# Attention and layer 1 of a graph network: two-part float32r tables beside another split of the mask and layernorm work

## The chip, the cores and the metric

One of the eight cores of a Trainium2 chip runs the whole program. Time is the device time of one execution in microseconds (us), and lower is better. A core has a matrix engine (TensorE, PE in the profile; its weight loads are PEld), a vector engine (VectorE, DVE), an activation engine (ScalarE, ACT), a general engine (GpSimd, POOL) and queues that issue transfers (SP, ACT and POOL).

## The reference

Sixteen graphs (B = 16) of 1024 nodes with 128 features pass through four layers, each with a residual addition and a layernorm. The change touches layers 0 and 1 and every layernorm.

```
# layer 0: masked attention
v = relu(x @ Wv.T + bv);  q = relu(x @ Wq.T + bq);  k = relu(x @ Wk.T + bk)
scores = einsum('bih,bjh->bij', q, k)
h = clip(scores * mask, 0.0, CLAMP_HI) - NEG_PENALTY * (1.0 - mask)
out = softmax(h, axis=2) @ v
# layer 1: maximum over the neighbours j of i
p = x @ (W1 - W2);  q = x @ W2
out = max_j relu(p[i] + q[j] + b) * adj[i, j]
# layer 2: a GIN layer.  layer 3: the adjacency is thinned row by row (dilation),
# then three SAGE layers with batch norms and a last linear map
# after each layer: x = layernorm(x + out)
```

The masks are the adjacency matrix itself, of zeros and ones. The thinning of layer 3 depends on the adjacency alone, and each row depends on the rows before it.

## The kernel before, in words

The program has two stages. The first, `layers_012`, computes layers 0 to 2 and, spread between their instructions, the thinning (`dilation`). The second, from the pools `xpool` and `sb` on, runs layer 3 batch by batch, four times over the sixteen graphs, and ends each graph with the last layernorm (called at L594).

In the first stage the outer loop runs over the graphs b. The spine of it is `max_conv(b)`, layer 1. A maximum over neighbours isn't a matrix product, so the kernel makes it one by tables. The 1024 neighbours are cut into 147 groups of seven (`NG`, `GS`). For each group, VectorE builds all 128 maxima over subsets of the seven values of `q`, for 21 groups at a time (`sub`, L270); TensorE transposes three groups at a time into `pt` (L277), and ScalarE copies them out as `table` (L279). The product of `lit` and the adjacency (`pm`, L284, bf16) tells which subset each node has as neighbours, and ScalarE turns it into a one-hot matrix `hot` (L286). The product of table and `hot` picks the maximum (`product`, L150, called by `look_up`, two halves of 512 columns in float32), and VectorE folds it into `best` (L262). So there are 16 x 147 = 2352 look-ups. A look-up is written one group late: `pm` and `hot` of group g stand before the look-up of group g-1. `pm` has one buffer of two PSUM banks, `pg` shares two such buffers with the other wide products.

After each group `between(g)` is called. It advances three generators. `dilation` gets 1400 pieces spread evenly over the 2352 groups: in each of eight blocks of 128 rows, 16 pieces that bring the block's rows up to date (a load of `E` by GpSimd's queue, L340; transposes and comparisons, L353 and L354), 127 steps of some ten small VectorE instructions that each need the one before (L374 to L387), 16 counts on ScalarE (L396), and 16 ranks (a scan of 1024 elements on VectorE, L413, an activation, L414, and a comparison, L416). `gin(b-1)`, layer 2, advances in the first 30 groups. `attention(b+1)`, layer 0, advances every tenth group from 40 on, one tile of 128 rows at a time.

One attention tile does this: GpSimd makes `off`, one where there is no edge (L219, bf16, from the adjacency rows `An`). TensorE multiplies q with the negated k (L222; GpSimd negates `kT` at L207) and adds 2^100 times `off` by a bf16 product with the diagonal matrix `penalty` (L223). VectorE clips and takes the row minimum in one instruction (L227), ScalarE takes the exponential (L229), TensorE transposes and multiplies with v, and VectorE scales and adds the residual (L242).

`layernorm` (L153 on) takes statistics of eight tiles on VectorE (L156), combines their halves by nine small GpSimd instructions (L161 to L169, the last a power), and normalises by eight GpSimd instructions (L171). It is called three times per graph in the first stage and once per graph at the end.

A scheduler orders each engine's instructions when the program is built; it follows program order where nothing stands against it. Each engine then runs its own in that order.

Of the kernel before, what the change touches and what calls it, by code (L numbers as in the profile page):

```python
# [23 lines left out]

F32 = mybir.dt.float32
BF = mybir.dt.bfloat16
U8 = mybir.dt.uint8  # L30
AF = mybir.ActivationFunctionType
ALU = mybir.AluOpType
# [4 lines left out]
P = 128  # L37
# [6 lines left out]
LOWEST = -(2.0**100)  # L44
MAGIC = 2.0**23
CLAMP_HI = 90000000000000.0
PENALTY = 2.0**100
LN_EPS = 1e-5


# [11 lines left out]
def tile_graph_layers(ctx: ExitStack, tc, a, out):  # L62
# [9 lines left out]
    def wide(name, tag="wide", bufs=2):  # L72
        return psum.tile([P, N], F32, tag=tag, name=name, bufs=bufs)

# [5 lines left out]
    make_identity(nc, ident)  # L80
    ident_b = consts.tile([P, P], BF, name="ident_b")
    make_identity(nc, ident_b)
    penalty = consts.tile([P, P], BF, name="penalty")
    nc.vector.tensor_scalar_mul(penalty, ident, PENALTY)
    ones = consts.tile([P, P], F32, name="ones")
    nc.vector.memset(ones, 1.0)
    ones_b = consts.tile([P, P], BF, name="ones_b")
# [31 lines left out]
    nc.vector.tensor_scalar_add(eps1, eps1, 1.0)  # L119


    mask_u = consts.tile([B, N], U8, name="mask_u")
    nc.sync.dma_start(out=mask_u, in_=a["nodemask"])
    half_mask = consts.tile([B, N], F32, name="half_mask")
    nc.vector.tensor_scalar(half_mask, mask_u, 0.5, None, op0=ALU.mult)
    nm = consts.tile([P, T, B], F32, name="nm")
    half_nm = consts.tile([P, T, B], F32, name="half_nm")
    pm = bank("pm")
# [23 lines left out]

    def layernorm(dst, src):  # L153
        st = small.tile([P, T, 6], F32, name="ln_st")
        for t in range(T):
            nc.vector.bn_stats(out=st[:, t, :], in_=src[:, t, :])  # L156

        mv = small.tile([P, 4, T], F32, name="ln_mv")
        mean, apart, var, rs = (mv[:, i, :] for i in range(4))
        gp = nc.gpsimd  # L160
        gp.tensor_add(mean, st[:, :, 1], st[:, :, 4])  # L161
        gp.tensor_sub(apart, st[:, :, 1], st[:, :, 4])  # L162
        gp.tensor_scalar(mean, mean, 0.5, None, op0=ALU.mult)  # L163
        gp.tensor_mul(apart, apart, apart)  # L164
        gp.tensor_add(var, st[:, :, 2], st[:, :, 5])  # L165
        gp.tensor_scalar(var, var, 1.0 / D, LN_EPS, op0=ALU.mult, op1=ALU.add)  # L166
        gp.tensor_scalar(apart, apart, 0.25, None, op0=ALU.mult)  # L167
        gp.tensor_add(var, var, apart)  # L168
        gp.tensor_tensor(rs, var, mhalf, op=ALU.pow)  # L169
        for t in range(T):  # L170
            gp.tensor_scalar(dst[:, t, :], src[:, t, :], mean[:, t:t + 1], rs[:, t:t + 1],  # L171
                             op0=ALU.subtract, op1=ALU.mult)

    def split(pool, src, left):

# [17 lines left out]
    def layers_012():  # L193
# [6 lines left out]
        def attention(b, An):  # L200
# [3 lines left out]
            kT = w4.tile([P, N], F32, name="kT")  # L204
            for w, bias, dst in ((WqT, bq, qT), (WkT, bk, kT)):
                nc.scalar.activation(dst, product(w, xT, "pqk"), AF.Relu, bias=bias)
            nc.gpsimd.tensor_scalar_mul(kT, kT, -1.0)  # L207
            v = w4.tile([P, T, D], F32, name="v")
            pv = wide("pv").rearrange("p (t d) -> p t d", d=D)
            for t in range(T):  # L210
# [3 lines left out]
            yield  # L214
            y = w4.tile([P, T, D], F32, name="y")
            for t in range(T):

                off = w4.tile([P, N], BF, name="off", tag="pen")
                nc.gpsimd.tensor_scalar(off, An[:, t, :], -1.0, 1.0, op0=ALU.mult, op1=ALU.add)  # L219
                psc = wide("psc")  # L220
                for s in halves:
                    nc.tensor.matmul(psc[:, s], qT[:, t * P:(t + 1) * P], kT[:, s], start=True, stop=False)  # L222
                    nc.tensor.matmul(psc[:, s], penalty, off[:, s], start=False, stop=True)  # L223
                e = w4.tile([P, N], F32, name="e", bufs=2)

                top = small.tile([P, 1], F32, name="top")
                nc.vector.tensor_scalar(e, psc, -CLAMP_HI, None, op0=ALU.max, op1=ALU.min, accum_out=top)  # L227
                total = small.tile([P, 1], F32, name="total")
                nc.scalar.activation(e, e, AF.Exp, bias=top, scale=-1.0, accum_out=total)  # L229
                eT = w4.tile([P, T, P], F32, name="eT")  # L230
                for h in range(2):
                    p = bank("pe")
                    for c in range(4):
                        nc.tensor.transpose(p[:, c * P:(c + 1) * P],
                                            e[:, (4 * h + c) * P:(4 * h + c + 1) * P], ident)
                    nc.scalar.copy(eT[:, 4 * h:4 * h + 4, :].rearrange("p c i -> p (c i)"), p)
                pav = bank("pav")
                for c in range(T):
                    nc.tensor.matmul(pav[:, :D], eT[:, c, :], v[:, c, :], start=(c == 0), stop=(c == T - 1))
                share = small.tile([P, 1], F32, name="share")  # L240
                nc.vector.reciprocal(share, total)
                nc.vector.scalar_tensor_tensor(y[:, t, :], pav[:, :D], share, X[b][:, t, :],  # L242
                                               op0=ALU.mult, op1=ALU.add)
                yield
# [3 lines left out]
        def max_conv(b, AT, between):  # L248
# [5 lines left out]
            qg = q.rearrange("o (g s) -> o g s", s=GS)  # L254
            best = w4.tile([P, N], F32, name="best")

            def look_up(g, table, hot):
                pg = product(table, hot, "pg")
                if g == 0:
                    nc.vector.tensor_copy(best, pg)  # L260
                else:
                    nc.vector.tensor_max(best, best, pg)  # L262

            last = None
            for g0 in range(0, NG, TG):
# [6 lines left out]
                for g in range(g0, g0 + TG):  # L272
                    at = (g - g0) % 3
                    if at == 0:
                        pt = bank("pt")
                        for k in range(3):
                            nc.tensor.transpose(pt[:, k * P:(k + 1) * P], sub[:, g - g0 + k, :], ident)  # L277
                        table = w2.tile([P, 3, P], F32, name="table", bufs=3)
                        nc.scalar.copy(table.rearrange("s g o -> s (g o)"), pt[:, :3 * P])  # L279
                    c, r = divmod(g, GC)  # L280
                    rows = min(CH, N - c * CH)
                    pm = wide("pm", "subset", 1)
                    for s in halves:
                        nc.tensor.matmul(pm[:, s], lit[:rows, r, :], AT[:rows, c, s], start=True, stop=True)  # L284
                    hot = w2.tile([P, N], F32, name="hot", bufs=2)
                    nc.scalar.activation(hot, pm, AF.Relu, bias=one_less)  # L286
                    if last is not None:
                        look_up(*last)
                    last = g, table[:, at, :], hot
                    between(g)  # L290
            look_up(*last)
            nc.vector.tensor_add(best, best, product(Wd, xT, "pp"))
# [43 lines left out]
        def dilation():  # L336
            for k in range(T):
# [32 lines left out]
                for n in range(P - 1):  # L370
                    mine = Dg[:, n, :]
                    m = slice(k * P + n, k * P + n + 1)
                    rank1 = small.tile([B, P], F32, name="rank1")
                    nc.vector.tensor_tensor_scan(rank1, mine, mine, before[:, n:n + 1], op0=ALU.add, op1=ALU.max)  # L374
                    sc = small.tile([B, 5], F32, name="sc")
                    half, h1, at, every, at2 = (sc[:, i:i + 1] for i in range(5))
# [3 lines left out]
                    nc.vector.scalar_tensor_tensor(at, half, 5.5, h1, op0=ALU.is_gt, op1=ALU.mult)  # L380
                    nc.vector.scalar_tensor_tensor(every, half, 1.0, at, op0=ALU.is_gt, op1=ALU.is_gt)
                    nc.vector.tensor_scalar(at2, at, 2.0, -1.0, op0=ALU.mult, op1=ALU.add)
                    hit = small.tile([B, P], F32, name="hit")
                    nc.vector.tensor_scalar(hit, rank1, at, every, op0=ALU.is_equal, op1=ALU.max)  # L384
                    nc.vector.scalar_tensor_tensor(hit, rank1, at2, hit, op0=ALU.is_equal, op1=ALU.max)  # L385
                    nc.vector.tensor_mul(hit, hit, mine)
# [236 lines left out]
```

## Time and profile before

| | |
|---|---|
| median of 3 runs | 9722.24 us (9721.92 to 9728.73) |
| the profiled execution | 9721.92 us |
| its span, first to last instruction | 9720.1 us |
| PE busy | 8365.7 us (86%), 29288 instructions |
| DVE busy | 7624.2 us (78%), 16197 instructions |
| ACT busy | 4286.9 us (44%), 5170 instructions |
| POOL busy | 1095.8 us (11%), 1423 instructions |
| mean granted TensorE clock | 0.932 |
| end of the loop over max_conv | about 7816 us |

Busy time counts an engine's instructions once where they overlap. A product in float32 shows as two records for each 512 columns (so L150 has 9408 for the look-ups). [...]records of one line overlap; the distance of their starts is the better price. A group of instructions is given with its count, its busy time, the mean of one in ns, and the idle time of the engine before them with what ended it. A wait is given as the engine and line that waited, the engine and line it waited for, the total in us, how often, and the longest.

### The profile page before, as it was taken

What the parts mean: (1) busy time and instruction counts of PE and PEld (TensorE: products, weight loads), DVE (VectorE), ACT (ScalarE), POOL (GpSimd) and SP (SyncE); (2) the same over time, 40 slices, a digit from 0 to 9 for tenths busy, and PEclk for the clock granted to TensorE, in tenths of its full rate; (3) what the DMA queues carried; (4) which work ended last, traced back from release to release, by engine and by line L of the source; (5) the groups of instructions that cost most, each with busy time, mean ns of one, the idle gap of its engine ahead of it and who ended that gap; (6) DMA issues with size and microseconds to landing.
All of it is one profiled execution on the core that took longest, in us unless ns stands there. A gap on an engine that the chain in (4) does not pass through costs nothing. (4 is left out here: it accounts for less than half of the span.)

```text
span 9720.1 us, 86636 instructions
## 1 busy us (share of the span) xinstructions
PE 8365.7 (86%) x29288; PEld 4084.1 (42%) x29288; DVE 7624.2 (78%) x16197; ACT 4286.9 (44%) x5170; POOL 1095.8 (11%) x1423
## 2 busy tenths in 40 slices
PE   7989898999899989898989898989898967778774
PEld 4444444444444444444444444444444433334333
DVE  4998599869886988699859986998699958845454
ACT  3445544554465445444554455445544621122221
POOL 1010101010101010101010101010101010101116
PEclk8999999999999999999999999999999978889886
DMA  3010201020102010201020102010200057733332
GB/s 47 1 22 19 35 1 22 19 37 1 22 20 39 1 22 20 40 1 22 19 43 1 22 18 46 1 22 18 47 1 11 11 159 201 200 115 130 130 130 75
DMA packets 317237, 435.20 MB, mean 45 GB/s; under 512 B 105445, under 2 KB 156792, under 8 KB 316662
## 3 DMA queue, kind: packets, MB, share of 16 engines
q1 hardware_dynamic: 219696, 295.75, 9.2%
q0 software_dynamic: 92560, 132.72, 8.8%
q8 instruction: 230, 3.77, 0.2%
q10 hardware_dynamic: 4534, 1.19, 0.1%
q14 instruction: 217, 1.78, 0.1%
HBM read 461.64 MB, written 119.54 MB: 60 GB/s over the span
## 5 line engine op out<-in xcount | busy, mean ns | idle before, releaser
L150 PE MATMUL pg<-hot,table 128*128 128x512 f32 x9408 | 4548.7, 605 | 134.4 <-DVE best L262 42.8
L286 ACT ACTIVATE hot<-pm,one_less 128x1024 f32<-128x1024 f32 x2352 | 2617.1, 1113 | 2235.1 <-PE pm L284 2080.4
L262 DVE TENSOR_TENSOR best<-best,pg 128x1024 f32<-128x1024 f32 x2336 | 2828.8, 1211 | 534.5 <-PE pg L150 530.4
L150 PEld LDWEIGHTS pg<-hot,table 128*128 128x128 f32 x9408 | 1729.4, 191 | 1770.3 <-issue 1137.5
L284 PE MATMUL pm<-AT,lit 126*128 126x512 bf16 x4704 | 1437.2, 385 | 190.9 <-ACT hot L286 101.3
L284 PEld LDWEIGHTS <-lit 126*128 126x128 bf16 x4704 | 461.0, 99 | 1099.8 <-issue 1067.1
L279 ACT COPY table<-pt 128x384 f32<-128x384 f32 x784 | 373.3, 477 | 816.5 <-PE pt L277 811.5
L219 POOL TENSOR_SCALAR off<-An 128x1024 bf16<-128x1024 bf16 x128 | 164.2, 1283 | 3578.7 <-PE psc L223 3183.0
L277 PE MATMUL pt<-ident,sub 128*128 128x128 f32 x2352 | 410.8, 283 | 178.3 <-DVE sub L270 88.6
L189 PE MATMUL pagg<-m,part 128*128 128x512 bf16 x2304 | 529.0, 382 | 34.9 <-DVE inv L530 25.4
L277 PEld LDWEIGHTS pt<-ident,sub 128*128 128x128 f32 x2352 | 304.4, 146 | 516.6 <-issue 270.2
L374 DVE TENSOR_TENSOR_SCAN rank<-Dg,before 16x128 f32<-16x128 uint8 x1016 | 498.4, 491 | 27.2
L270 DVE TENSOR_TENSOR sub<-sub,q 128x21 f32<-128x21 f32 (+6 forms) x784 | 434.9, 555 | 49.3 <-ACT q L252 43.9
L387 DVE TENSOR_TENSOR Dg<-Dg,hit 16x127 uint8<-16x127 uint8 (+63 forms) x1016 | 454.2, 447 | 24.5
L189 PEld LDWEIGHTS <-part 128*128 128x128 bf16 x3072 | 298.2, 98 | 394.9 <-issue 53.4
L385 DVE SCALAR_TENSOR_TENSOR hit<-rank,sc,hit 16x128 f32<-16x128 f32 x1016 | 348.1, 343 | 25.6
L557 PE MATMUL pl<-w_L_gnn_Wl,hT 128*128 128x128 f32 x768 | 199.1, 367 | 178.6 <-ACT hT L581 113.2
L178 ACT CAST part<-left 128x1024 bf16<-128x1024 f32 x128 | 133.7, 1044 | 482.9 <-DVE left L180 482.8
L384 DVE TENSOR_SCALAR hit<-rank,sc 16x128 f32<-16x128 f32 x1016 | 342.7, 337 | 0.0
L532 DVE RECIPROCAL inv<-inv 128x1024 f32<-128x1024 f32 x48 | 314.3, 6548 | 19.3 <-ACT inv L531 19.3
L560 DVE SCALAR_TENSOR_TENSOR x<-pl,nm,x 128x128 f32<-128x128 f32 x384 | 129.5, 337 | 252.2 <-PE pl L557 161.4
L171 POOL TENSOR_SCALAR X<-y,ln_mv 128x128 f32<-128x128 f32 x384 | 319.4, 848 | 5.2
(172 smaller groups left out, 8512.2 us busy)
## 6 DMA issues: line engine op xcount, KB each, us to landing
m<-kept SPq DMA_DIRECT2D x32, 2048.0 KB, 9.4
An<-in_adj_dram POOLq DMA_DIRECT2D x16, 2048.0 KB, 14.3
removed<-gone SPq DMA_DIRECT2D x128, 256.0 KB, 2.0
m<-in_adjT_dram POOLq DMA_DIRECT2D x16, 2048.0 KB, 13.6
gone_all<-removed SPq DMA_DIRECT2D x16, 2048.0 KB, 9.7
kept<-m SPq DMA_DIRECT2D x16, 2048.0 KB, 14.2
AT<-in_adjT_dram POOLq DMA_DIRECT2D x16, 2016.0 KB, 14.6
hidden<-r SPq DMA_DIRECT2D x48, 512.0 KB, 3.8
```

The costliest lines, as they stand in the source:

```text
L150: nc.tensor.matmul(p[:, s], lhsT, rhs[:, s], start=True, stop=True)
L189: nc.tensor.matmul(p[:, s], parts[k][:, c, :], m[:, c, s], start=(c == 0 and k == 0), stop=(c == T - 1 and k == 2))
L262: nc.vector.tensor_max(best, best, pg)
L270: nc.vector.tensor_max(sub[:, :, n:2 * n], sub[:, :, 0:n], qg[:, g0:g0 + TG, k:k + 1].to_broadcast([P, TG, n]))
L277: nc.tensor.transpose(pt[:, k * P:(k + 1) * P], sub[:, g - g0 + k, :], ident)
L279: nc.scalar.copy(table.rearrange("s g o -> s (g o)"), pt[:, :3 * P])
L284: nc.tensor.matmul(pm[:, s], lit[:rows, r, :], AT[:rows, c, s], start=True, stop=True)
L286: nc.scalar.activation(hot, pm, AF.Relu, bias=one_less)
L374: nc.vector.tensor_tensor_scan(rank1, mine, mine, before[:, n:n + 1], op0=ALU.add, op1=ALU.max)
L384: nc.vector.tensor_scalar(hit, rank1, at, every, op0=ALU.is_equal, op1=ALU.max)
L385: nc.vector.scalar_tensor_tensor(hit, rank1, at2, hit, op0=ALU.is_equal, op1=ALU.max)
L387: nc.vector.tensor_tensor(Dg[:, n + 1:, n], Dg[:, n + 1:, n], hit[:, n + 1:], op=ALU.is_gt)
```

## The change

- `look_up`: the table of three groups is kept in two float32r parts. ScalarE copies `pt` out twice, once to `high` (float32r) and once to `whole` (float32); GpSimd subtracts them to give `low` (float32r). `hot` is float32r. For each half of 512 columns two float32r products, with `high` and `low`, add up in `pg`, in place of one float32 product. `high` and `low` have two buffers, `whole` one; `table` had three.
- attention: `penalty`, the bf16 product with it, `off` and the negation of `kT` go. GpSimd makes a float32 `pen` from `An`. VectorE clips and multiplies by `An` in one instruction, adds `pen` in a second, and takes the negated row maximum in a third.
- `layernorm`: a bn_aggr per tile on VectorE in place of GpSimd's combination of halves; GpSimd keeps one addition and the power; the normalisation of the eight tiles is on VectorE.
- the node mask is loaded by a GpSimd transfer that converts to float32; `rank1` and `hit` have two buffers in place of three.

```
@@ -26,6 +27,7 @@
 from concourse.masks import make_identity
 
 F32 = mybir.dt.float32
+F32R = mybir.dt.float32r
 BF = mybir.dt.bfloat16
 U8 = mybir.dt.uint8
 AF = mybir.ActivationFunctionType
@@ -44,7 +46,7 @@
 LOWEST = -(2.0**100)
 MAGIC = 2.0**23
 CLAMP_HI = 90000000000000.0
-PENALTY = 2.0**100
+NEG_PENALTY = 9000000000000000.0
 LN_EPS = 1e-5
 
 
@@ -80,8 +82,6 @@
     make_identity(nc, ident)
     ident_b = consts.tile([P, P], BF, name="ident_b")
     make_identity(nc, ident_b)
-    penalty = consts.tile([P, P], BF, name="penalty")
-    nc.vector.tensor_scalar_mul(penalty, ident, PENALTY)
     ones = consts.tile([P, P], F32, name="ones")
     nc.vector.memset(ones, 1.0)
     ones_b = consts.tile([P, P], BF, name="ones_b")
@@ -119,10 +119,9 @@
     nc.vector.tensor_scalar_add(eps1, eps1, 1.0)
 
 
-    mask_u = consts.tile([B, N], U8, name="mask_u")
-    nc.sync.dma_start(out=mask_u, in_=a["nodemask"])
     half_mask = consts.tile([B, N], F32, name="half_mask")
-    nc.vector.tensor_scalar(half_mask, mask_u, 0.5, None, op0=ALU.mult)
+    nc.gpsimd.dma_start(out=half_mask, in_=a["nodemask"])
+    nc.vector.tensor_scalar(half_mask, half_mask, 0.5, None, op0=ALU.mult)
     nm = consts.tile([P, T, B], F32, name="nm")
     half_nm = consts.tile([P, T, B], F32, name="half_nm")
     pm = bank("pm")
@@ -152,24 +151,16 @@
 
     def layernorm(dst, src):
         st = small.tile([P, T, 6], F32, name="ln_st")
+        mv = small.tile([P, T, 2], F32, name="ln_mv")
+        rs = small.tile([P, T], F32, name="ln_rs")
         for t in range(T):
             nc.vector.bn_stats(out=st[:, t, :], in_=src[:, t, :])
-
-        mv = small.tile([P, 4, T], F32, name="ln_mv")
-        mean, apart, var, rs = (mv[:, i, :] for i in range(4))
-        gp = nc.gpsimd
-        gp.tensor_add(mean, st[:, :, 1], st[:, :, 4])
-        gp.tensor_sub(apart, st[:, :, 1], st[:, :, 4])
-        gp.tensor_scalar(mean, mean, 0.5, None, op0=ALU.mult)
-        gp.tensor_mul(apart, apart, apart)
-        gp.tensor_add(var, st[:, :, 2], st[:, :, 5])
-        gp.tensor_scalar(var, var, 1.0 / D, LN_EPS, op0=ALU.mult, op1=ALU.add)
-        gp.tensor_scalar(apart, apart, 0.25, None, op0=ALU.mult)
-        gp.tensor_add(var, var, apart)
-        gp.tensor_tensor(rs, var, mhalf, op=ALU.pow)
+            nc.vector.bn_aggr(out=mv[:, t, :], in_=st[:, t, :])
+        nc.gpsimd.tensor_scalar(rs, mv[:, :, 1], LN_EPS, None, op0=ALU.add)
+        nc.gpsimd.tensor_tensor(rs, rs, mhalf, op=ALU.pow)
         for t in range(T):
-            gp.tensor_scalar(dst[:, t, :], src[:, t, :], mean[:, t:t + 1], rs[:, t:t + 1],
-                             op0=ALU.subtract, op1=ALU.mult)
+            nc.vector.tensor_scalar(dst[:, t, :], src[:, t, :], mv[:, t, 0:1], rs[:, t:t + 1],
+                                    op0=ALU.subtract, op1=ALU.mult)
 
     def split(pool, src, left):
 
@@ -204,7 +195,6 @@
             kT = w4.tile([P, N], F32, name="kT")
             for w, bias, dst in ((WqT, bq, qT), (WkT, bk, kT)):
                 nc.scalar.activation(dst, product(w, xT, "pqk"), AF.Relu, bias=bias)
-            nc.gpsimd.tensor_scalar_mul(kT, kT, -1.0)
             v = w4.tile([P, T, D], F32, name="v")
             pv = wide("pv").rearrange("p (t d) -> p t d", d=D)
             for t in range(T):
@@ -214,19 +204,17 @@
             yield
             y = w4.tile([P, T, D], F32, name="y")
             for t in range(T):
-
-                off = w4.tile([P, N], BF, name="off", tag="pen")
-                nc.gpsimd.tensor_scalar(off, An[:, t, :], -1.0, 1.0, op0=ALU.mult, op1=ALU.add)
-                psc = wide("psc")
-                for s in halves:
-                    nc.tensor.matmul(psc[:, s], qT[:, t * P:(t + 1) * P], kT[:, s], start=True, stop=False)
-                    nc.tensor.matmul(psc[:, s], penalty, off[:, s], start=False, stop=True)
+                psc = product(qT[:, t * P:(t + 1) * P], kT, "psc")
+                pen = w4.tile([P, N], F32, name="pen")
+                nc.gpsimd.tensor_scalar(pen, An[:, t, :], -1.0, NEG_PENALTY, op0=ALU.add, op1=ALU.mult)
                 e = w4.tile([P, N], F32, name="e", bufs=2)
 
+                nc.vector.scalar_tensor_tensor(e, psc, CLAMP_HI, An[:, t, :], op0=ALU.min, op1=ALU.mult)
+                nc.vector.tensor_add(e, e, pen)
                 top = small.tile([P, 1], F32, name="top")
-                nc.vector.tensor_scalar(e, psc, -CLAMP_HI, None, op0=ALU.max, op1=ALU.min, accum_out=top)
+                nc.vector.tensor_reduce(top, e, axis=mybir.AxisListType.X, op=ALU.max, negate=True)
                 total = small.tile([P, 1], F32, name="total")
-                nc.scalar.activation(e, e, AF.Exp, bias=top, scale=-1.0, accum_out=total)
+                nc.scalar.activation(e, e, AF.Exp, bias=top, accum_out=total)
                 eT = w4.tile([P, T, P], F32, name="eT")
                 for h in range(2):
                     p = bank("pe")
@@ -254,8 +242,11 @@
             qg = q.rearrange("o (g s) -> o g s", s=GS)
             best = w4.tile([P, N], F32, name="best")
 
-            def look_up(g, table, hot):
-                pg = product(table, hot, "pg")
+            def look_up(g, parts, hot):
+                pg = wide("pg")
+                for s in halves:
+                    for k, part in enumerate(parts):
+                        nc.tensor.matmul(pg[:, s], part, hot[:, s], start=(k == 0), stop=(k == 1))
                 if g == 0:
                     nc.vector.tensor_copy(best, pg)
                 else:
@@ -275,18 +266,22 @@
                         pt = bank("pt")
                         for k in range(3):
                             nc.tensor.transpose(pt[:, k * P:(k + 1) * P], sub[:, g - g0 + k, :], ident)
-                        table = w2.tile([P, 3, P], F32, name="table", bufs=3)
-                        nc.scalar.copy(table.rearrange("s g o -> s (g o)"), pt[:, :3 * P])
+                        high = w2.tile([P, 3 * P], F32R, name="high", bufs=2)
+                        nc.scalar.copy(high, pt[:, :3 * P])
+                        whole = w2.tile([P, 3 * P], F32, name="whole")
+                        nc.scalar.copy(whole, pt[:, :3 * P])
+                        low = w2.tile([P, 3 * P], F32R, name="low", bufs=2)
+                        nc.gpsimd.tensor_sub(low, whole, high.bitcast(F32))
                     c, r = divmod(g, GC)
                     rows = min(CH, N - c * CH)
                     pm = wide("pm", "subset", 1)
                     for s in halves:
                         nc.tensor.matmul(pm[:, s], lit[:rows, r, :], AT[:rows, c, s], start=True, stop=True)
-                    hot = w2.tile([P, N], F32, name="hot", bufs=2)
+                    hot = w2.tile([P, N], F32R, name="hot", bufs=2)
                     nc.scalar.activation(hot, pm, AF.Relu, bias=one_less)
                     if last is not None:
                         look_up(*last)
-                    last = g, table[:, at, :], hot
+                    last = g, [t[:, at * P:(at + 1) * P] for t in (high, low)], hot
                     between(g)
             look_up(*last)
             nc.vector.tensor_add(best, best, product(Wd, xT, "pp"))
@@ -370,7 +365,7 @@
                 for n in range(P - 1):
                     mine = Dg[:, n, :]
                     m = slice(k * P + n, k * P + n + 1)
-                    rank1 = small.tile([B, P], F32, name="rank1")
+                    rank1 = small.tile([B, P], F32, name="rank1", bufs=2)
                     nc.vector.tensor_tensor_scan(rank1, mine, mine, before[:, n:n + 1], op0=ALU.add, op1=ALU.max)
                     sc = small.tile([B, 5], F32, name="sc")
                     half, h1, at, every, at2 = (sc[:, i:i + 1] for i in range(5))
@@ -380,7 +375,7 @@
                     nc.vector.scalar_tensor_tensor(at, half, 5.5, h1, op0=ALU.is_gt, op1=ALU.mult)
                     nc.vector.scalar_tensor_tensor(every, half, 1.0, at, op0=ALU.is_gt, op1=ALU.is_gt)
                     nc.vector.tensor_scalar(at2, at, 2.0, -1.0, op0=ALU.mult, op1=ALU.add)
-                    hit = small.tile([B, P], F32, name="hit")
+                    hit = small.tile([B, P], F32, name="hit", bufs=2)
                     nc.vector.tensor_scalar(hit, rank1, at, every, op0=ALU.is_equal, op1=ALU.max)
                     nc.vector.scalar_tensor_tensor(hit, rank1, at2, hit, op0=ALU.is_equal, op1=ALU.max)
                     nc.vector.tensor_mul(hit, hit, mine)
```

## Prediction before the run

> **What bounds the kernel now.** I read the page's slices first, then the stretches, then two timelines, then the waits. Columns of the first fence: stretch, its length, then busy time (and instructions) of PE, PEld, DVE, ACT, POOL, then clock and DMA.
>
> ```profile
> 1175.00:1811.00 636.00, 585.70 (x1946) 279.10 (x1945) 593.98 (x1617) 291.59 (x328) 52.39 (x67) 0.97 0.04 9
> 980.00:1175.00 195.00, 171.83 (x571) 82.39 (x570) 98.37 (x136) 100.64 (x154) 34.74 (x56) 0.91 0.28 42
> 1829.00:1952.00 123.00, 104.76 (x348) 50.54 (x347) 105.16 (x97) 82.73 (x106) 6.47 (x3) 0.97 0.10 34
> 9530.00:9720.00 190.00, 80.77 (x256) 60.39 (x256) 76.02 (x264) 20.25 (x17) 154.49 (x275) 0.51 0.28 86
> ```
>
> The loop over max_conv ends at about 7816 us. The dilation cuts it into eight blocks of four phases, whose borders I took from the starts of L374 (first of 127 row steps) and L413 (16 ranks). The first row is a step phase: VectorE is busy 593.98 of 636 us. The second is a load phase (from the last rank to the first step): VectorE 50%, TensorE 88%. The third is a rank phase. The fourth is the end of the program: GpSimd 81%. Summed over the eight blocks: step 5104 us with 1594 of the 2352 subset groups, load 1537 us (422), rank 985 us (295), count 137 us (41).
>
> In the step phases VectorE is full: 4769 us busy, and 206 us more are gaps under 0.1 us between instructions that depend on each other. Only 130 us are longer gaps. TensorE is 92% busy there too, but it isn't alone in setting the pace.
>
> A timeline in a load phase (start, length, instruction):
>
> ```profile
> 1004.70 0.60 PE L284 MATMUL pm<-AT,lit 126*128 126x512 bf16 x2
> 1005.13 1.88 PE L150 MATMUL pg<-hot,table 128*128 128x512 f32 x4
> 1005.39 1.11 ACT L286 ACTIVATE hot<-pm,one_less 128x1024 f32<-128x1024 f32 x1 [1.04 <-PE pm L284]
> 1005.57 0.19 PEld L150 LDWEIGHTS pg<-hot,table 128*128 128x128 f32 x1 [0.24 <-issue]
> 1006.00 0.19 PEld L150 LDWEIGHTS pg<-hot,table 128*128 128x128 f32 x1 [0.24 <-issue]
> 1006.85 0.38 PE L284 MATMUL pm<-AT,lit 126*128 126x512 bf16 x1
> ```
>
> A group takes 2.15 us: 0.43 for the two bf16 products, 1.72 for the look-up, whose four records are 0.43 apart. ScalarE waits 1.04 us per group for `pm`. The three transposes of every third group add 0.33 us (1002.22 to 1002.55), so 2.25 us on average: TensorE sets this phase.
>
> ```profile
> DVE best L262 <- PE pg L150: 530.4, 469, 6.0
> ```
>
> ```profile
> L262 DVE TENSOR_TENSOR best<-best,pg 128x1024 f32<-128x1024 f32 x2336 | 2828.8, 1211 | 534.5 <-PE pg L150 530.4
> L227 DVE TENSOR_SCALAR_CACHE_REDUCE e<-psc 128x1024 f32<-128x1024 f32 x128 | 156.3, 1221 | 31.5 <-PE psc L223 31.5
> L180 DVE TENSOR_TENSOR left<-left,part 128x1024 f32<-128x1024 f32 x64 | 77.8, 1216 | 17.8 <-ACT part L178 17.8
> L384 DVE TENSOR_SCALAR hit<-rank,sc 16x128 f32<-16x128 f32 x1016 | 342.7, 337 | 0.0
> L171 POOL TENSOR_SCALAR X<-y,ln_mv 128x128 f32<-128x128 f32 x384 | 319.4, 848 | 5.2
> L169 POOL TENSOR_TENSOR ln_mv<-ln_mv,mhalf 128x8 f32<-128x8 f32 x64 | 107.2, 1674 | 5.0
> ```
>
> That line of the waits is the whole of what VectorE loses to the look-up: 530 us. Most of it lies in the load phases (some 390 us); 37 in the steps, 93 in the ranks, 9 in the counts. The rows of the groups (busy, mean ns, idle before) are prices used below.
>
> **What the Trainium skill says.** "FP8 and Floating Point Precision", section TensorE Precision Notes: a true float32 product is four passes, the reduced-precision one a single read cut to a shorter format. The trace agrees on the first half: 0.86 us for a 512-column float32 product against 0.215 for bf16. No float32r product runs here. "SBUF — State Buffer", section Who interferes with whom: VectorE with two SBUF inputs, or in a two-port mode, and a GpSimd instruction that reads SBUF lock each other out for whole instructions. The trace agrees: VectorE instructions that overlap L219 or L207 on GpSimd run over their usual time by 0.28 us per L219 (1.28 us long) and 0.63 us per L207 (2.83 us), about 0.22 us for each us of GpSimd. "VectorE: DVE Perf Modes", the perf-mode tier table: a reduce, and a float32 operation on two tensors, run at one element per cycle. L180 agrees with 1.216 us for 1024; no tensor_reduce is in the trace.
>
> **The look-up.** Four float32 products' records of 0.43 us become four float32r products of 0.215 us (taken at bf16's rate, the single pass of the page): 1.72 to 0.86 us per group, some 2000 us of TensorE in all. It isn't all collected. `pm` has one buffer, so the next `pm` follows the last `hot`: from `pm`'s start to `hot` 0.69 us, `hot` 1.11, about 0.08 to the next `pm`: 1.88 us. `high` and `whole` (0.477 us each, from the row of L279) push one `hot` in three back by about 0.25: 1.96 us a group. So a load-phase group goes from 2.25 to 1.96: 422 x 0.29 = **-122 us** (none if the load phases are set by their batch borders, -363 if the whole 0.86 comes through). In the step, rank and count phases only VectorE's long waits can go: 295 us at most, of which I take the 139 for `pg`: **-140 us**.
>
> **The low part on GpSimd.** 784 subtractions of 128x384. The two-input L535 takes 2.11 us for 1024 at its shortest and L161 0.21 for 8, so 0.9 us each. It is hidden by the group between (3 us), but its read locks VectorE: 0.9 x 0.22 = 0.2 us. The 1930 groups of the VectorE-full phases have 643: **+129 us** (0 to 260, since it has two inputs). The second copy on ScalarE adds 373 us to an engine at 44%; step phases hide it.
>
> **Attention.** Per tile VectorE loses L227 with its accumulator read (1.296 us) and gains a mask product from PSUM (1.21, as L262), an addition (1.216, L180) and a reduce (1.22, estimate from the tier table and L180; at least 1.07 at one element per cycle), with two dependent starts of 0.04: 3.73, or +2.43. By the positions of L227, 15 of 128 tiles lie in load phases, where the idle half of VectorE covers them (else 36 us more). 113 x 2.43 = **+275 us**. The removed bf16 mask products and `penalty` free TensorE where it isn't needed; the sign change of `kT` goes. `pen` replaces `off` on GpSimd, priced between L219 (1.05 us) and L207 (2.8): **+9 us** of lock after what `off` and `kT` cost.
>
> **Layernorm.** VectorE gets eight bn_aggr (0.18 each, between its 0.14 us floor and bn_stats' 0.28), loses the overlap of bn_stats (0.15 with the wait), and gets eight normalisations (0.30, from L384's 0.337 less overlap): 5.0 us. It then waits for GpSimd's addition and power (0.25 + 1.67); I take half of that as filled by other work: 6.0 us, bounds 3.5 to 8. By L156's positions 30 of the loop's 48 lie in VectorE-full phases: **+180 us**. At a batch border the chain bn_stats to X (11.7 us at 1051.8) becomes some 9, and the longer table chain gives 1.6 of it back: nothing. At the end GpSimd's period of 9.9 us per batch gives way to VectorE's 8 to 8.5: **-25 us**.
>
> The mask load by GpSimd and the two-buffer `rank1` and `hit`: nothing, the load is before the loop and the steps are serial; at worst a few us.
>
> **Sum.** -122 - 140 + 129 + 275 + 9 + 180 - 25 = +306. The profiled execution took 9721.9 us (span 9720.1 and 1.8 around it), which is the median of the runs (9722.2) within 0.4. So 9722 + 306 = **10028 us**; own range 9830 to 10260 from the bounds, not all at one end.
>
> **Rivals.** (1) Faster: TensorE's freed time decides. In the load phases the whole 0.86 us comes through (-363), all 295 us of long waits go, and the lock costs nothing: 275 + 9 + 180 - 363 - 295 - 25 = -219, 9503 us. It decides once these gains pass 464 us. For it: TensorE is at 88 to 92%; against it: one `pm` buffer, and 97% of the step phases is VectorE work or its short gaps. (2) GpSimd becomes a link: `low` stands in order behind `pen`, which waits for VectorE's addition, and behind the layernorm's power, which waits for bn_aggr; the look-up stands behind `low`. At 2 us for each of 128 tiles and 48 layernorms: +352, 10380 us. For it: GpSimd already stands in line 3183 us at L219; against: other work fills VectorE. (3) float32r isn't a single pass. With half the float32 rate per pass nothing is saved and both gains go: 9722 + 464 + 129 - 25 = 10290 us. At the full float32 price a look-up gains 1.72 us: +4000 us.
>
> **Chances.** Forecast 0.60, GpSimd 0.17, float32r 0.10 (0.03 of it four passes), faster 0.13. The range 9720 to 10400 leaves out the faster case nearly whole, the four passes and some of the GpSimd case. 0.2% is about what a measurement of this kernel tells from no change. Faster 0.13, same 0.03, slower 0.84.
>
> **What will show it.** Right: four float32r records of about 0.21 us per group; step phases longer, at 650 to 700 us per block, with VectorE near 97% and TensorE under 70%; load phases shorter; longer L374, L385 and L387 beside `low`; three rows of about 1.2 us in attention. Wrong: VectorE with long waits for `pg` in the step phases (GpSimd), or step phases no longer than 636 us (rival 1).

## The result, and the profile after

The changed kernel takes 10017.0 us (median of 4 runs, 10001.2 to 10019.5) where the kernel before takes 9722.9 us beside it: a ratio of 1.0298 (95% interval 1.0280 to 1.0316), or +294 us. The forecast was 10028 us. The sum was close, but its parts weren't: three were off by 125 us or more, and the errors cancelled.

Four stretches of the profile after, answering to those of before (stretch, length, busy time and instructions of PE, PEld, DVE, ACT, POOL, then clock and DMA): a step phase, a load phase, a rank phase, the end.

```profile
1170.00:2001.00 831.00, 637.46 (x2619) 399.06 (x2617) 773.47 (x1861) 437.65 (x546) 121.41 (x120) 0.91 0.05 10
1087.00:1170.00 83.00, 47.51 (x204) 29.68 (x204) 39.70 (x79) 46.42 (x101) 11.71 (x12) 0.77 0.32 40
2011.00:2107.00 96.00, 20.05 (x73) 9.21 (x74) 61.94 (x42) 39.24 (x53) 2.27 (x2) 0.57 0.32 68
9827.00:10017.00 190.00, 90.03 (x280) 64.40 (x280) 126.45 (x529) 22.84 (x19) 33.41 (x35) 0.54 0.28 89
```

The step phase has grown from 636 to 831 us and now holds 273 look-ups and not 197. VectorE is still at 93%, TensorE has fallen from 92 to 77%. The load phase has shrunk from 195 to 83 us, and in the rank phase TensorE is busy for only 21%: 3 look-ups stand beside a block's 16 ranks, against 37 before. That order was made when the program was built. The program text still spreads the dilation evenly over the groups; the order built does not keep to that, so the scheduler is less bound to program order than I had written ahead of the prediction. At the end VectorE has taken GpSimd's place as the busiest engine (126.45 against 33.41 us).

The look-ups also finish before the dilation does. In the kernel before, the last `hot` and the last rank end within 2 us of each other, at about 7815 us. After, the last `hot` ends at 7955 us and the last rank at 8184. The dilation's last 39 steps and 16 ranks stand alone there, with VectorE busy for 73%:

```profile
7955.00:8184.00 229.00, 39.84 (x129) 20.90 (x128) 166.90 (x498) 43.00 (x57) 3.96 (x4) 0.55 0.18 61
```

The mean granted TensorE clock is 0.856 after, and it was 0.932. It is lowest where TensorE has little to do (0.57 in the rank phase above, 0.91 in the step phase). Of the look-up's products that follow one another within 0.6 us, 337 of 7030 start in a stretch of half clock, so the look-up itself meets little of it.

A timeline of the look-up after:

```profile
1127.79 0.59 PE L279 MATMUL pm<-AT,lit 126*128 126x512 bf16 x2 [0.68 <-ACT hot L281]
1128.22 0.19 PEld L249 LDWEIGHTS pg<-hot,low 128*128 128x128 f32 x1
1128.46 0.19 PEld L249 LDWEIGHTS pg<-hot,high 128*128 128x128 f32 x1
1128.69 0.19 PEld L249 LDWEIGHTS pg<-hot,low 128*128 128x128 f32 x1
1129.91 0.59 PE L279 MATMUL pm<-AT,lit 126*128 126x512 bf16 x2 [0.27 <-ACT hot L281]
```

A float32r product of 512 columns takes 0.23 us (the distance of the weight loads), where 0.215 was forecast, and the next `pm` waits for ScalarE's `hot`, as forecast: 2.12 us from one `pm` to the next, where I took 1.96.

The groups that the change made (count, then busy us, mean ns of one, idle before):

```profile
L253 DVE TENSOR_TENSOR best<-best,pg 128x1024 f32<-128x1024 f32 x2336 | 2843.9, 1217 | 208.7 <-PE pg L249 194.1 <-DVE sc L375 0.4 <-DVE sc L372 0.3
L212 DVE SCALAR_TENSOR_TENSOR e<-psc,An 128x1024 f32<-128x1024 f32 x128 | 158.1, 1235 | 20.7 <-PE psc L149 17.8 <-PE pe L222 2.0
L213 DVE TENSOR_TENSOR e<-e,pen 128x1024 f32<-128x1024 f32 x128 | 157.0, 1226 | 0.6
L215 DVE TENSOR_REDUCE top<-e 128x1 f32<-128x1024 f32 x128 | 153.2, 1197 | 0.0
L158 DVE BATCH_NORM_AGGREGATE ln_mv<-ln_st 128x2 f32<-128x6 f32 x512 | 85.5, 172 | 0.4
L380 DVE SCALAR_TENSOR_TENSOR hit<-rank,sc,hit 16x128 f32<-16x128 f32 x1016 | 382.1, 376 | 17.7
```

The three attention rows cost what was priced (1.235, 1.226 and 1.197 us). The last row is an instruction of the dilation's steps whose work the change leaves as it was. It was 343 ns before:

```profile
L385 DVE SCALAR_TENSOR_TENSOR hit<-rank,sc,hit 16x128 f32<-16x128 f32 x1016 | 348.1, 343 | 25.6
```

and is 376 now. e4 and e9 below show that this comes from GpSimd's subtraction.

Waits of VectorE after:

```profile
DVE best L253 <- PE pg L249: 194.1, 253, 4.3
DVE E L349 <- DMA E<-in_adj_dram: 180.9, 7, 26.6
DVE gone L411 <- ACT rank L409: 158.7, 121, 1.4
DVE half L395 <- ACT junk L391: 115.7, 8, 14.5
DVE rank L408 <- DMA E<-own: 59.3, 8, 8.0
```

The wait for the look-up has fallen from 530 to 194 us. Four other waits, all inside the dilation, have come up: 515 us together. Before, the wait of `gone` for `rank` was 26 us and the other three were too short for the list. A wait of layer 2, `left` for ScalarE's cast `part`, has fallen from 182 to 29 us (56 in e3, 153 in e1). Of before:

```profile
DVE left L180 <- ACT part L178: 181.8, 34, 12.2
DVE gone L416 <- ACT rank L414: 26.4, 66, 1.6
```

### The profile page after: what moved, and what is told of

Same layout as the page of the kernel before. It is cut to its first block, busy times and chain, and to the rows that moved or that the text cites. A ratio compares the mean times of both kernels' runs of the same rounds, so it can differ in the third digit from the quotient of the medians.

```text
span 10017.0 us, 88548 instructions
## 1 busy us (share of the span) xinstructions
PE 6938.9 (69%) x29032; PEld 4206.2 (42%) x29032; DVE 8181.0 (82%) x17348; ACT 4586.5 (46%) x5954; POOL 1307.7 (13%) x1232
## 5 line engine op out<-in xcount | busy, mean ns | idle before, releaser
L281 ACT ACTIVATE hot<-pm,one_less 128x1024 fp32r<-128x1024 f32 x2352 | 2623.9, 1116 | 1897.8 <-PE pm L279 1644.4
L253 DVE TENSOR_TENSOR best<-best,pg 128x1024 f32<-128x1024 f32 x2336 | 2843.9, 1217 | 208.7 <-PE pg L249 194.1
L249 PE MATMUL pg<-hot,high 128*128 128x512 f32 x4704 | 2269.6, 488 | 164.8 <-DVE best L253 58.9
L249 PE MATMUL pg<-hot,low 128*128 128x512 f32 x4704 | 1905.7, 411 | 89.3 <-POOL low L274 89.0
L274 POOL TENSOR_TENSOR low<-whole,high 128x384 fp32r<-128x384 f32 x784 | 800.9, 1022 | 4513.7 <-ACT whole L272 4342.1
L249 PEld LDWEIGHTS pg<-hot,high 128*128 128x128 f32 x4704 | 911.9, 196 | 635.4 <-DVE best L253 140.7
L249 PEld LDWEIGHTS pg<-hot,low 128*128 128x128 f32 x4704 | 926.2, 197 | 317.2 <-POOL low L274 154.4
L348 PE MATMUL pr<-ident_b,rp 128*128 128x128 bf16 x448 | 54.5, 250 | 950.6 <-DVE E L349 498.5
L270 ACT CAST high<-pt 128x384 fp32r<-128x384 f32 x784 | 373.9, 477 | 545.0 <-PE pt L268 463.4
L348 PEld LDWEIGHTS <-rp 128*128 128x128 bf16 x448 | 36.0, 112 | 913.1 <-DMA rp<-removed 458.5
L272 ACT COPY whole<-pt 128x384 f32<-128x384 f32 x784 | 382.9, 488 | 67.0 <-POOL low L274 65.5
```

What stands on the lines that cost most here:

```text
L249: nc.tensor.matmul(pg[:, s], part, hot[:, s], start=(k == 0), stop=(k == 1))
L272: nc.scalar.copy(whole, pt[:, :3 * P])
L274: nc.gpsimd.tensor_sub(low, whole, high.bitcast(F32))
```

## The experiments

Each difference is taken against the kernel before in the same session. The account beside it comes from each trace: the loop reaches from the first `hot` to the last `hot` or rank, and VectorE's busy time in it is a union.

| kernel | us | against before | loop | VectorE busy | idle | after the loop |
|---|---|---|---|---|---|---|
| before | 9722.9 | | 7764 | 6509 | 1255 | 1904 |
| changed | 10017.0 | +294 | 8131 | 7033 | 1099 | 1833 |
| e1_tables | 9839.2 | +119 | 7951 | 6685 | 1266 | 1833 |
| e2_attention | 9923.8 | +204 | 7953 | 6723 | 1230 | 1917 |
| e3_norm | 9641.1 | -79 | 7702 | 6610 | 1092 | 1888 |
| e4_low_twice | 10310.7 | +591 | 8438 | 7254 | 1183 | 1820 |
| e5_low_by_product | 9785.3 | +66 | 7887 | 6761 | 1126 | 1834 |
| e6_product_norm | 9456.0 | -264 | 7562 | 6532 | 1029 | 1829 |
| e7_token | 10034.5 | +315 | 8119 | 7094 | 1026 | 1859 |
| e8_all | 9651.1 | -69 | 7724 | 6614 | 1110 | 1876 |
| e9_tables_product | 9592.3 | -135 | 7696 | 6444 | 1252 | 1843 |
| e10_tables_norm | 9724.4 | -3 | 7842 | 6772 | 1070 | 1833 |
| e11_normalise_only | 9720.9 | -6 | 7762 | 6600 | 1161 | 1909 |
| e12_aggregate_only | 9676.9 | -50 | 7730 | 6537 | 1194 | 1885 |

**One part at a time.** My theory was that VectorE's work decides, with some of TensorE's freed time coming in as well; the rival was that the freed time decides. The edits of e1, e2 and e3 are the hunks of the diff for `look_up` with its tables, for `attention`, and for `layernorm`. e1 also takes the hunks for the node mask, `rank1` and `hit`, for the room that the tables need; what these cost alone no run shows.

> The kernel before with the two-part float32r tables alone (and the room that they need: the node mask loaded by GpSimd, rank1 and hit in two buffers); attention and layernorm as before. Theory A (VectorE's work decides, and the order in which the scheduler places the dilation follows the tables): take VectorE's measured extra work off the changed kernel: attention 128 x 2.43 = 311 us, layernorm 48 x 5 = 240 us, and give back 20 us at the end: about 9490 us. The ranks then stand nearly alone, as in the changed kernel (about 3 look-ups during a block's 16 ranks, against 37 before). Theory B (my phases as predicted: -122 -140 +129): about 9590 us, with ranks still between look-ups. Rival (freed TensorE time comes through whole, 0.86 us in every group of the load phases and all long waits): about 9170 us.

Measured 9839 us, ratio 1.0121 (1.0104 to 1.0138): slower than before, and no forecast had it. The rival falls. Theory A's order came true, its time didn't: it leaned on prices for attention and layernorm that e2 and e3 don't bear out. VectorE's idle time in the loop is 1266 us, and it was 1255. The freed TensorE time bought nothing there, and VectorE had 176 us more to do. The look-ups did end earlier, the last `hot` at 7770 us and not at 7814, but 232 us of dilation were then left.

> The kernel before with the attention edit alone: VectorE makes three passes per tile in place of one. VectorE-bound: 113 of 128 tiles lie where VectorE is full, 113 x 2.43 = +275 us, up to +311 if all count, about 10000 to 10030 us. If TensorE shared the bound, the removed bf16 mask products (128 x 0.43 = 55 us) come back: about 9950 us. If TensorE alone bounded: 9670 us.

Measured 9924 us, ratio 1.0205 (1.0190 to 1.0221): below the first two forecasts and 254 us above the third. The nearest, 9950 us, has TensorE share the bound, but the trace puts the difference on VectorE. Its idle time fell by only 25 us. Its busy time rose by 214 us and not by 275 to 311: the three passes less the one that they replace fill 285 us more of the loop, and VectorE's other work fills 71 us less. The lock of `off` and `kT`, which goes, explains some 40 of these 71; the rest stays open.

> The kernel before with the layernorm edit alone. VectorE-bound: +180 us in the loop, -25 us at the end, about 9880 us. If VectorE had room: -25 to -80 us (a shorter chain at the batch borders and the end), about 9670 us.

Measured 9641 us, ratio 0.9916 (0.9901 to 0.9930): faster, which was the alternative's sign. VectorE's busy time rose by 101 us and its idle time fell by 163. Two timelines of a batch border show how. First before, then e3:

```profile
1051.80 1.64 DVE L156 BATCH_NORM_STATS2 ln_st<-y 128x6 f32<-128x128 f32 x8
1055.45 1.68 POOL L169 TENSOR_TENSOR ln_mv<-ln_mv,mhalf 128x8 f32<-128x8 f32 x1
1057.24 6.27 POOL L171 TENSOR_SCALAR X<-y,ln_mv 128x128 f32<-128x128 f32 x8
```

```profile
1042.60 0.48 DVE L158 BATCH_NORM_STATS2 ln_st<-y 128x6 f32<-128x128 f32 x2
1044.94 0.24 POOL L160 TENSOR_SCALAR ln_rs<-ln_mv 128x8 f32<-128x8 f32 x1 [10.25 <-DVE ln_mv L159]
1045.27 1.67 POOL L161 TENSOR_TENSOR ln_rs<-ln_rs,mhalf 128x8 f32<-128x8 f32 x1
1046.97 2.14 DVE L163 TENSOR_SCALAR X<-y,ln_mv,ln_rs 128x128 f32<-128x128 f32 x8 [2.12 <-POOL ln_rs L161]
```

From the first statistics to the last normalised tile it is 11.7 us before and 6.5 us in e3. Eight pairs of statistics and bn_aggr take 2.3 us, and the eight normalisations 2.14 us, 0.27 each.

**The lock.**

```
                         nc.gpsimd.tensor_sub(low, whole, high.bitcast(F32))
+                        nc.gpsimd.tensor_sub(low, whole, high.bitcast(F32))
```

> The changed kernel with GpSimd's subtraction for the low part issued twice (same result). Lock theory: in the changed trace VectorE instructions beside one subtraction run 0.40 us over their usual time; twice as many subtractions give 784 x 0.40 = +314 us less what falls where VectorE idles: +230 to +314 us, seen as longer small VectorE instructions. Link theory (GpSimd's queue holds up the look-up): the wait of the low product for GpSimd, 89 us now, grows by about 1 us for every third group, up to several hundred us, with VectorE idle. Neither: no change.

Measured 10311 us, +297 on the changed kernel: inside the lock theory's range. The order of look-ups, steps and ranks is that of the changed kernel. The small instruction of the steps in e4:

```profile
L381 DVE SCALAR_TENSOR_TENSOR hit<-rank,sc,hit 16x128 f32<-16x128 f32 x1016 | 420.2, 414 | 17.5
```

and in e9, where GpSimd makes no low part:

```profile
L397 DVE SCALAR_TENSOR_TENSOR hit<-rank,sc,hit 16x128 f32<-16x128 f32 x1016 | 347.9, 342 | 22.0
```

343, 376 and 414 ns with none, one and two subtractions per table, and 342 with none again. The median is 338 or 339 ns in all four: a few instructions run long, and the others not at all. Of the 1016, those over the median by a quarter number 15 before, 63 after, 126 in e4 and 7 in e9. The fold into `best`, one of whose inputs is in PSUM, hardly changes: 1211, 1217, 1217 and 1213 ns. Of the 297 us, 221 are VectorE's busy time and 84 its idle time, less 13 after the loop. So the queue of GpSimd has a share too: the low product's wait for it rose from 89 to 324 us. After, then e4:

```profile
PE pg L249 <- POOL low L274: 89.0, 165, 1.1
PE pg L249 <- POOL low L275: 323.8, 211, 3.5
```

**The order.** After the first runs I thought that the gain was lost because ranks, counts and loads now stand alone, with VectorE idle for 664 us in them.

```
                     nc.vector.tensor_mul(hit, hit, mine)
+                    if n % 8 == 7:
+                        nc.vector.scalar_tensor_tensor(one_less[:B], hit[:, 0:1], 0.0, one_less[:B], op0=ALU.mult, op1=ALU.add)
```

> The changed kernel with one thing added: every eighth step of the dilation writes the bias that the one-hot activation reads (its own value plus zero times a step's result), so that look-ups can't be ordered ahead of the dilation. By the order built, a block's 16 ranks then stand among 45 look-ups and not among 3; the 120 extra VectorE instructions cost about 20 us. Order theory (the freed TensorE time was lost because ranks, counts and loads of the dilation stand alone, with VectorE idle 664 us in them): VectorE's idle time in the loop falls from 1100 to some 750 us, about 9690 us. Rival (that idle time belongs to the serial dilation whatever stands beside it): 10020 to 10040 us.

Measured 10034 us, 21 us more than the changed kernel: the rival's time. A step phase and a rank phase of e7:

```profile
1155.00:1880.00 725.00, 521.56 (x2088) 323.50 (x2087) 673.85 (x1712) 346.91 (x438) 97.08 (x95) 0.88 0.04 9
1895.00:2045.00 150.00, 108.86 (x404) 69.91 (x403) 120.71 (x135) 98.40 (x131) 28.10 (x21) 0.84 0.13 26
```

and its largest wait:

```profile
DVE best L253 <- PE pg L249: 308.9, 259, 11.2
```

The ranks have company again (VectorE 80% there, not 65%), and the waits inside the dilation have shrunk (`E` for its load from 181 to 30 us, `gone` for `rank` from 159 to 26). The wait for `pg` came back, from 194 to 309 us. Idle time fell by 73 us, not by 350, and busy time rose by 61: most of the idle time had changed its name and place. So my order theory didn't hold as it stood, and the rival's reason, that this idle time belongs to the dilation, isn't shown either. The run isn't a clean test: the added dependence holds up the look-ups itself (ScalarE waits 659 us for `one_less`), and a gain from the order may be hidden under its cost.

**The low part without GpSimd.** e5 does this in the changed kernel, with `minus` the negative unit matrix in float32r; the two ScalarE copies stay two.

```
-                        whole = w2.tile([P, 3 * P], F32, name="whole")
-                        nc.scalar.copy(whole, pt[:, :3 * P])
+                        rest = bank("rest")
+                        for k in range(3):
+                            at_k = slice(k * P, (k + 1) * P)
+                            nc.tensor.matmul(rest[:, at_k], sub[:, g - g0 + k, :], ident, start=True, stop=False)
+                            nc.tensor.matmul(rest[:, at_k], minus, high[:, at_k], start=False, stop=True)
                         low = w2.tile([P, 3 * P], F32R, name="low", bufs=2)
-                        nc.gpsimd.tensor_sub(low, whole, high.bitcast(F32))
+                        nc.scalar.copy(low, rest[:, :3 * P])
```

> The changed kernel with the low part made by TensorE (the table's transpose once more in float32, minus the high part by a product with the negative unit matrix) and copied out by ScalarE; GpSimd's subtraction and the copy whole go. Lock theory: the 317 us by which VectorE instructions ran long beside the subtractions go, 9700 us at the old order. By the order built, the ranks also stand among 36 look-ups again; if the order theory holds too, some 300 us more: about 9400 us. If neither: 10020 us, TensorE having 784 x 0.9 us more to do.

Measured 9785 us, 228 less than the changed kernel: VectorE's busy time fell by 272 us. The lock's share came, though the time is 85 us above the lock theory's 9700. The order's share didn't: in the trace the ranks of a block but the last stand among 34 to 36 look-ups again, without any added dependence, and VectorE's idle time in the loop is 1126 us, where it was 1099. TensorE has more to do here, so this test isn't quite clean either.

> The kernel before with tables in two parts, the low part by TensorE, and the layernorm edit; attention as before. From the runs so far: e5's forecast less attention's 204 to 311 us: about 9150 us, below both kernels. VectorE's work of before in the loop is 6508 us, layernorm's 100 more, idle some 700, start and layer 3 1885: 9190 us. If order and lock don't add up: 9400 us.

> The same with the added dependence of look-ups on the dilation's steps. The order is already good without it, so the 120 instructions and the tighter coupling cost 0 to 40 us: about 9180 us.

e6, the tables of e5 and the layernorm edit on the kernel before, took 9456 us, ratio 0.9728 (0.9713 to 0.9742): faster than both kernels, though 300 us short of my forecast, which still counted on the order. e8 adds the dependence of e7 and took 9651 us: the tighter coupling costs 195 us there, five times the most I allowed. VectorE waits 156 us of that kernel's load phases for a cast of X on ScalarE (23 in e6, and 23 in e7), and ScalarE waits 271 us for the dependence. Why it costs so much more than in e7 stays open.

**The account closed.** e9 is e6 without the layernorm edit, e10 the changed kernel without the attention edit.

> The kernel before with the two-part tables, the low part by TensorE and ScalarE (as in e5), attention and layernorm as before: the tables without GpSimd's lock. Account of VectorE (loop time is VectorE's busy time plus an idle time that stayed between 1025 and 1265 us in all kernels so far): e6's 9456 us plus the 79 us that the layernorm edit saved alone: 9535 us, so the freed TensorE time is worth some 185 us and the lock in e1 some 300. If the lock is not what made e1 slower: 9840 us.

> The changed kernel with the attention edit undone. If the parts add up: e1's 9839 less 79 = 9760 us; taking attention's 204 us off the changed kernel gives 9813 us. If attention costs its full 128 x 2.43 us where all tiles lie in VectorE-full stretches: 9706 us.

e9 took 9592 us, ratio 0.9854 (0.9838 to 0.9871): the tables without GpSimd are worth -135 us, and with it +119, so GpSimd's subtraction costs 254; that is 57 us above the 9535 forecast and far from 9840. e10 took 9724 us, ratio 0.9992 (0.9984 to 1.0001), nearest to the last of its three forecasts, so the parts don't quite add: layernorm is worth -122 beside the tables (-79 alone), attention +297 (+204 alone).

**The halves of layernorm.** In e11 only the last loop goes to VectorE; in e12 only the statistics change.

```
-            gp.tensor_scalar(dst[:, t, :], src[:, t, :], mean[:, t:t + 1], rs[:, t:t + 1],
+            nc.vector.tensor_scalar(dst[:, t, :], src[:, t, :], mean[:, t:t + 1], rs[:, t:t + 1],
```

> The kernel before with only the normalisation of the eight tiles moved from GpSimd to VectorE; GpSimd still combines the statistics. Border theory (the layernorm edit gains because the chain at each batch border falls from 11.7 to 6.5 us): this half takes 6.3 us of GpSimd's down to 2.1, some 4 us per border and per last-layer graph: -60 us, less 8 x 0.2 us of VectorE's work per layernorm: 9650 to 9690 us. If VectorE's work alone counts: 9720 + 48 x 2 = 9820 us.

> The kernel before with only the statistics moved: bn_aggr on VectorE, two instructions on GpSimd in place of nine; GpSimd still normalises. Border theory: the chain loses about 1 us (nine GpSimd instructions 3.7 us, two take 2.0, bn_aggr adds 0.7): -15 us at the borders, -20 at the end, less VectorE's bn_aggr 48 x 0.7 = 34: 9710 us, within 20 us of no change. If VectorE's work alone counts: 9720 + 48 x 1.4 = 9790 us.

e11 took 9721 us (ratio 0.9993, 0.9986 to 0.9999), e12 9677 us (0.9944, 0.9929 to 0.9958). Both border forecasts missed, in opposite directions. Normalising on VectorE saved 94 us of idle time and cost 91 us of work. The statistics saved 61 us of idle time and 19 at the end, for 28 us of work. Idle savings and work add up to nearly those of e3 (155 against 163 us, 119 against 101).

The border theory is right in part. Between the start of a layernorm's last statistics and the end of its last normalised tile, VectorE idles 176 us before, summed over the loop's 46 layernorms; it is 122 in e11, 141 in e12 and 78 in e3. A little over half of the idle time that each edit saves lies there (54 of 94, 35 of 61, 98 of 163 us). Where the rest lies no run shows.

## Why the prediction was right in its sum, point by point

Adding the edits one by one (e9, e1, e10, changed) gives -135 + 254 - 122 + 297 = +294. Against the prediction's steps:

- **The look-up, -122 and -140 forecast.** This step failed. Without the lock the tables gave -135, and none of it from VectorE's idle time in the loop: 1255 us before, 1252 in e9, 1266 in e1. Of e9's gain, 61 us came after the loop, where less work was left over, and 65 are busy time of VectorE, most of it in the small instructions of the steps; why these take less stays open. The price of the product was nearly right (0.23 us), and so was the limit by `pm` and `hot`. What was wrong is that a shorter group shortens the phase. In e9 the load phases fall from 1537 to 1090 us, but they hold 222 look-ups and not 422, and the step phases grow from some 5100 to 5510 us. In the order as built the faster look-ups run ahead of the dilation, and VectorE waits for the dilation's own chain in place of `pg`. In e7, which limits the running ahead, the wait for `pg` comes back. That no order could keep the gain isn't shown.
- **The low part on GpSimd, +129 forecast.** The mechanism was right and the size wrong. VectorE instructions beside a subtraction ran 0.40 us over, not 0.20 (317 us over 784), and e1 against e9 gives 254 us in all. The price came from one-input GpSimd instructions; this one has two inputs, for which I had kept 260 us as the upper end. The Trainium skill's "SBUF — State Buffer", section Who interferes with whom, has a VectorE instruction with two inputs in SBUF contend with a GpSimd instruction that reads SBUF, and not one with at most a single input there outside its two-port modes. That fits what e4 and e9 show of `hit` (L385) and of `best`. The one-input `hit` before it ran over too (337 ns before, 370 after); whether it is in a two-port mode no trace here tells.
- **Attention, +275 and +9 forecast.** The sum was right: +297 beside the tables. The three rows cost what was priced. The 9 us for the lock had the wrong sign: by the time that VectorE instructions beside them run over, `off` and `kT` cost 36 and 10 us before, and `pen` 5 us after. Alone the edit was +204. VectorE's work differs by 47 us between the two (261 against 214). The lock of `off` and `kT` doesn't explain that, since it goes in both (it is 42 us in e10); the difference stays open.
- **Layernorm, +180 forecast.** This step failed in its sign. In e3 VectorE's work rose by 101 us in the loop, not by 5 us for each of 48. The normalisation took 0.27 us, near its price, and fills 97 us of the loop. bn_aggr fills 38, or 0.8 us per layernorm, where I had taken 2.6 for it and for the lost overlap of bn_stats: the pairs overlap too. VectorE's other work is 33 us less. And the batch border, put at nothing, was worth most: the chain is 6.5 us and not 9, and 98 of the 163 us of idle time that went lay in such chains. The wait for GpSimd's power, 105 us in e3 (78 for `X` and 27 for `y`), is inside these numbers.
- **The end, -25 forecast.** From the first store to the last it is 140.1 us and 148.6 before: -8.5. A graph takes 9.3 us in the mean (6.4 and 12.9 in turn), not 8 to 8.5. In e12, where GpSimd still normalises, it takes 8.4.
- **GpSimd as a link.** Only in part: the low product waits 89 us for GpSimd after, while VectorE waits less for `pg` than before.
- **What was to show it.** Products of about 0.21 us, longer steps beside the subtraction and three attention rows: right. Step phases of 650 to 700 us with TensorE under 70%: wrong, 786 to 831 us and 76%; they hold more look-ups, because the order changed.

In sum, the forecast was too hopeful by 127 us for the tables, too low by 125 for the lock and too high by some 280 for layernorm with the end; attention took up the rest. That the median came within 11 us is luck in the errors. That the kernel is slower rests on VectorE's work, which grew by 524 us in the loop, while its idle time there fell by 156 and the time after the loop by 71.

Open: why VectorE's idle time in the loop stays between 1026 and 1266 us in all fourteen kernels, whichever engine it waits for. The dilation's serial chain beside the batch borders may be the reason; no run removed it.

## What to carry to other kernels

When one engine is nearly full, account for a change in that engine's busy time first, and don't credit time freed on another engine until an experiment shows the wait gone and not renamed. A chain that many batches pass through is worth a timeline of its own, even when it takes 12 us. If an idle engine gets new work, ask whether it holds up the full engine, and price it also by what the full engine's instructions beside it lose.

## What the runs showed of the hardware

- A GpSimd subtraction of 128x384 with two inputs in SBUF takes 1.02 us and costs VectorE about 0.4 us here. The loss is uneven: the median of a small step instruction stays at 338 ns, and more of them run long.
- A TensorE product in float32r of 512 columns: 0.23 us; in float32 0.86 us.
- bn_aggr on two groups of statistics: 0.17 us. Pairs of bn_stats and bn_aggr follow each other at 0.26 us, where bn_stats alone follow at 0.2 us.
- tensor_reduce over 1024 float32 elements: 1.197 us.
